# A selective scan laid out as 16 states x 8 channels, with the other stages emitted between its units and the norms' 1/std taken for 8 chunks at once

## Chip, cores, metric

The kernel runs on one core of one Trainium2 chip. The metric is the device time of one launch in microseconds. Medians are over 4 to 9 runs, and the kernel before was run again on the same chip beside every group of experiments (medians 14344 to 14357 us). The engines are PE (TensorE, the matmuls), DVE (VectorE), ACT (ScalarE) and POOL (GpSimd). The granted clock is the share of TensorE's full clock that the trace records; in the traces each stretch of it has either 1.0 ("warm" below) or 0.5 ("cold"), and the numbers between are means over time. "Filling the array" below means 128 rows by 128 columns, the largest size that matmuls have in these traces.

## The reference, cut to what matters

Four images of 96 x 64 x 64 go through four layers: layer 0 is a gated block with a depthwise convolution and a selective scan in four directions, layer 1 a deformable convolution (gathers with bilinear weights), layer 2 a Fourier mixer and a quantized feed-forward block, layer 3 linear attention and another feed-forward block. The scan is:

```python
def selective_scan(u, dts, A, Bs, Cs, D, delta_bias):
    delta = jax.nn.softplus(dts + delta_bias[None, :, :, None])
    ...
    def step(h, inp):
        d_t, u_t, b_t, c_t = inp
        dA = jnp.exp(d_t[..., None] * A)
        h = dA * h + (d_t * u_t)[..., None] * b_t[:, :, None, :]
        y = jnp.einsum('bkdn,bkn->bkd', h, c_t)
        return (h, y)
```

with 192 channels, 16 states, 4 directions and 4096 positions per image.

## The kernel before

It works layer after layer, and in layer 0 image after image. One unit of the scan is one state of 128 channels over 1024 positions (cut):

```python
for n in range(NS):
    bc = sp.tile([128, 2, T], F32, ..., bufs=4)        # B and C of state n, on all partitions
    ...
    nc.sync.dma_start(dst, src.partition_broadcast(dst.shape[0]))
    da = ps.tile([128, T], F32, ..., bufs=2)           # PSUM
    nc.scalar.activation(da, delta, AF.Exp, scale=a_n)
    db = sp.tile([128, T], F32, ..., bufs=2)           # SBUF
    nc.vector.tensor_mul(db, du, bc[:, 0, :])
    nc.vector.tensor_tensor_scan(along(hh), along(da), along(db), first, ALU.mult, ALU.add)
    ...
    nc.gpsimd.tensor_mul(hc, hh, bc[:, 1, :])
    for h in range(T // CH):                           # sum over the states, in PSUM
        nc.tensor.matmul(py[:, hs], lhsT=net.ident, rhs=hc[:, hs], start=(n == 0), stop=(n == NS - 1))
```

The norms take 1/std by a square root, a reciprocal on DVE and a Newton step, once per chunk of 512 positions, on 96 partitions.

Of the kernel before, what the change touches and what calls it, by code (L numbers as in the profile page):

```python
# [9 lines left out]
F32 = mybir.dt.float32  # L10
# [10 lines left out]
L = H * W  # L21
DI, NS, R, KG = 192, 16, 6, 4
D2 = DI - 128
T = 1024
NT = L // T
CH = 512
NCH = L // CH
PW = W + 2
GW = W + 3
GE = GW * GW  # L30

# Columns of "vecs", one small vector per column.
(V_ING, V_INB, V_CBA, V_CBC, V_DTA, V_DTC, V_DSA, V_DSC, V_OGA, V_OBA, V_OGC, V_OBC,
 V_L1B, V_BN2, V_F2B1, V_F2B2, V_BFF, V_F3B1, V_F3B2, V_OMB, NV) = (
    0, 1, 2, 3, 4, 8, 10, 14, 18, 19, 20, 21, 22, 23, 27, 30, 31, 32, 35, 36, 37)


# [1 line left out]
def prepare(x, **w):  # L39
# [14 lines left out]
    for k in range(KG):  # L54
        put(V_DTA + k, w["L0_conv_dt_b"][k, :128])
        put(V_DSA + k, w["L0_conv_Ds"].reshape(KG, DI)[k, :128])
        put(V_DSC + k, w["L0_conv_Ds"].reshape(KG, DI)[k, 128:])
    for p in range(2):
        put(V_DTC + p, np.concatenate([w["L0_conv_dt_b"][2 * p + q, 128:] for q in range(2)]))
# [13 lines left out]
    a["vecs"] = vecs  # L73

    # Layer 0. Tile "a": channels 0..127; tile "c": channels 128..191, twice.
    wi = w["L0_conv_in_proj_w"].T
    a["w_in"] = c(np.concatenate([wi[:, :128], wi[:, 128:192], wi[:, 128:192], wi[:, 192:]], axis=1))
    cw = w["L0_conv_conv_w"].reshape(DI, 9)
    a["cw"] = c(np.stack([cw[:128], np.concatenate([cw[128:], cw[128:]])], axis=1))
    xp = w["L0_conv_x_proj_w"]  # L80
    xp = np.concatenate([xp[:, R:], xp[:, :R]], axis=1).transpose(0, 2, 1)
    a["xp_a"] = c(xp[:, :128].transpose(1, 0, 2))
    a["xp_c"] = c(np.stack([np.concatenate([xp[2 * p, 128:], xp[2 * p + 1, 128:]]) for p in range(2)], axis=1))
    a["dtw"] = c(w["L0_conv_dt_w"].transpose(2, 0, 1))
    al = w["L0_conv_A_logs"].reshape(KG, DI, NS)
    a["al_a"] = c(al[:, :128].transpose(1, 0, 2))
    a["al_c"] = c(np.stack([np.concatenate([al[2 * p, 128:], al[2 * p + 1, 128:]]) for p in range(2)], axis=1))
# [4 lines left out]
    # Layer 1.  # L92
# [5 lines left out]
    a["wdc"] = c(w["L1_conv_weight"].reshape(C, C, 9).transpose(1, 2, 0))  # L98

    # Layers 2 and 3.  # L100
# [13 lines left out]
    # Constants of the shapes alone.  # L114
# [4 lines left out]
    # Centring of 192 channels: from 0..127, and from 128..191 as the lower or the upper half holds them.  # L119
    cen = (np.eye(DI) - 1.0 / DI).astype(f)  # L120
    a["cen_a"] = c(cen[:128])
    a["cen_lo"] = np.concatenate([cen[128:], np.zeros((64, DI), f)])
    a["cen_up"] = np.concatenate([np.zeros((64, DI), f), cen[128:]])
# [6 lines left out]
    def complex_matrix(z):  # L130
        # [k, ..., m] complex -> [(re, im) k, ..., (re, im) m] real
        re = np.concatenate([z.real, z.imag], axis=-1)
        im = np.concatenate([-z.imag, z.real], axis=-1)
        return np.concatenate([re, im], axis=0).astype(f)
# [16 lines left out]
class Net:  # L151
    def __init__(self, ctx, tc, ins):
        self.tc, self.nc, self.ins = tc, tc.nc, ins
        nc = self.nc
        self.const = ctx.enter_context(tc.tile_pool(name="const", bufs=1))
        self.vecs = self.load("vecs", self.const)
        self.ident = self.load("ident", self.const)
        self.cen96 = self.load("cen96", self.const)
        self.grp3 = self.load("grp3", self.const)
        self.mean96 = self.const.tile([96, 96], F32, name="mean96")  # L160
        nc.vector.memset(self.mean96, 1.0 / 96)
        self.eps = self.const.tile([128, 1], F32, name="eps")
        nc.vector.memset(self.eps, 1e-5)
        self.one = self.const.tile([128, 1], F32, name="one")
        nc.vector.memset(self.one, 1.0)

    def load(self, name, pool):
        src = self.ins[name]
        t = pool.tile(list(src.shape), F32, name="w_" + name)
        self.nc.sync.dma_start(t, src)  # L170
        return t
# [3 lines left out]

    def inv_sqrt(self, out, var, tmp, p):
        """out = 1 / sqrt(var + 1e-5) on p partitions. The square root's table is short of
        float32's precision, so a step of Newton's follows."""
        nc, eps = self.nc, self.eps[:p]
        nc.scalar.activation(out, var, AF.Sqrt, bias=eps)  # L180
        nc.vector.reciprocal(out, out)  # L181
        nc.scalar.activation(tmp, out, AF.Square)
        nc.vector.scalar_tensor_tensor(tmp, var, eps, tmp, ALU.add, ALU.mult)  # L183
        nc.gpsimd.tensor_scalar(tmp, tmp, -0.5, 1.5, ALU.mult, ALU.add)  # L184
        nc.gpsimd.tensor_mul(out, out, tmp)  # L185

    def group_norm_stats(self, x, pool, psum, key):
        """Per-channel mean and 1/std of x [96, 4096] over its group of three channels."""
# [6 lines left out]
        gm = psum.tile([C, 512], F32, name=f"gnps{key}", tag="lna")  # L195
# [6 lines left out]
        gv = psum.tile([C, 512], F32, name=f"gnpv{key}", tag="lnb")  # L202
# [4 lines left out]
    def layer_norm(self, out, x, pool, psum, key):  # L207
        """out = (x - mean) / sqrt(var + 1e-5) over the 96 channels (partitions) of x [96, 512]."""
        nc = self.nc
        cen = psum.tile([C, CH], F32, name=f"lnc{key}", tag="lna")  # L210
        nc.tensor.matmul(cen, lhsT=self.cen96, rhs=x, start=True, stop=True)  # L211
        sq = pool.tile([C, CH], F32, name=f"lnq{key}", tag="lnq")
        nc.scalar.activation(sq, cen, AF.Square)
        var = psum.tile([C, CH], F32, name=f"lnv{key}", tag="lnb")
        nc.tensor.matmul(var, lhsT=self.mean96, rhs=sq, start=True, stop=True)  # L215
        sd = pool.tile([C, CH], F32, name=f"lns{key}", tag="lns")
        nw = pool.tile([C, CH], F32, name=f"lnw{key}", tag="lnw")
        self.inv_sqrt(sd, var, nw, C)
        nc.vector.tensor_mul(out, cen, sd)  # L219


@with_exitstack
def layer0(ctx, net, x1):
    """Selective scan over four directions of each image, into x1."""
    tc, nc, ins = net.tc, net.nc, net.ins
    wp = ctx.enter_context(tc.tile_pool(name="l0w", bufs=1))
    w_in = net.load("w_in", wp)
    cw = net.load("cw", wp)
    xp_a = net.load("xp_a", wp)
    xp_c = net.load("xp_c", wp)  # L230
    wo_a = net.load("wo_a", wp)
    wo_c = net.load("wo_c", wp)
    cen_a, cen_lo, cen_up = (net.load(q, wp) for q in ("cen_a", "cen_lo", "cen_up"))
    dtw = wp.tile([2 * NS + R, KG, DI], F32, name="dtw")
    nc.sync.dma_start(dtw[2 * NS :], ins["dtw"])
    pos192 = wp.tile([128, 128], F32, name="pos192")
    nc.vector.memset(pos192, 1.0 / DI)
    # A = -exp(A_logs)
    nega = []
    for name, k in (("al_a", KG), ("al_c", 2)):  # L240
        t = net.load(name, wp)
        nc.scalar.activation(t, t, AF.Exp)
        nc.vector.tensor_scalar_mul(t, t, -1.0)
        nega.append(t)
    # The four directions' skip terms fall on the same pixel.
    dsum = wp.tile([128, 2], F32, name="dsum")
    nc.vector.reduce_sum(dsum[:, 0:1], net.vecs[:, V_DSA : V_DSA + 4], axis=mybir.AxisListType.X)
    nc.vector.reduce_sum(dsum[:, 1:2], net.vecs[:, V_DSC : V_DSC + 4], axis=mybir.AxisListType.X)
    scratch = ctx.enter_context(tc.tile_pool(name="l0d", bufs=1, space=DRAM))
    keep = ctx.enter_context(tc.tile_pool(name="l0keep", bufs=1))  # L250

    for b in range(B):
        xa = keep.tile([128, L], F32, name=f"xa{b}", tag="xa")
        xat = keep.tile([128, L], F32, name=f"xat{b}", tag="xat")
        xc = keep.tile([128, L], F32, name=f"xc{b}", tag="xc")
        ya = keep.tile([128, L], F32, name=f"ya{b}", tag="ya")
        yc = keep.tile([128, L], F32, name=f"yc{b}", tag="yc")
        z_d = scratch.tile([DI, L], F32, name=f"z{b}", tag="z", bufs=2)

        with tc.tile_pool(name=f"l0a{b}", bufs=1) as big, tc.tile_pool(  # L260
            name=f"l0b{b}", bufs=2
        ) as sm, tc.tile_pool(name=f"l0p{b}", bufs=2, space=PSUM) as ps:
            xg = big.tile([C, L], F32, name=f"xg{b}", tag="xg")
            nc.sync.dma_start(xg, ins["x"][b])
            xn_all = big.tile([C, L], F32, name=f"xn{b}", tag="xn")
            pads = []
            for g in range(2):
                t = big.tile([128, PW, PW], F32, name=f"pad{b}_{g}", tag=f"pad{g}")
                nc.gpsimd.memset(t, 0.0)
                pads.append(t)  # L270
            # The depthwise convolution's taps as diagonal matrices.
            diag = big.tile([128, 2, 9, 128], F32, name=f"diag{b}", tag="diag")
            for g in range(2):
                for q in range(9):
                    nc.vector.tensor_scalar_mul(diag[:, g, q, :], net.ident, cw[:, g, q : q + 1])
# [624 lines left out]
```

## Time and profile before

| | before |
|---|---|
| median, us | 14344.2 |
| granted clock, mean | 0.737 |
| busy: PE / DVE / ACT / POOL | 59% / 66% / 26% / 49% |
| scan of one image | 384 units, 4.84 us each (from the starts of DVE's scan instructions) |

The lines that carry this are in the prediction below. One more row of the groups matters later, the sum over the states on PE (its columns are busy us and mean ns of one, then idle time before it and what ended that):

```profile
L473 PE MATMUL py<-hc,w_ident 128*128 128x512 f32 x6144 | 3964.7, 787 | 2956.2 <-POOL hc L470 2954.9
```

These matmuls fill the array, 128 rows by 128 columns (128*128 in the row). In the scan the granted clock is 0.78 although PE is busy only 60% of it.

### The profile page before, as it was taken

To read this page: it belongs to the slowest core of one execution; us is meant where nothing else is said; L and a number is where in the kernel's file an instruction comes from. 1 tells how busy PE (TensorE), PEld (TensorE's weight loads), DVE (VectorE), ACT (ScalarE), POOL (GpSimd) and SP (SyncE) were. 2 spreads that over 40 slices of the span, in tenths; PEclk is the share of its full clock that TensorE was granted. 3 is DMA by queue.
4 is the path that set the end of the run, shared out by engine and by line. 5 is a ranking of instruction groups with operands and counts; after the bars stand their busy time and mean duration, and the time that the engine had idled before them with its cause. 6 is when DMAs were issued, how large, how long until landed. Compare 5 with 4: busy or idle time off the path is not lost. (4 is left out here: it accounts for less than half of the span.)

```text
span 14347.4 us, 74112 instructions
## 1 busy us (share of the span) xinstructions
PE 8526.9 (59%) x24048; PEld 3467.6 (24%) x24048; DVE 9414.3 (66%) x5970; ACT 3702.4 (26%) x5474; POOL 7050.9 (49%) x3392
## 2 busy tenths in 40 slices
PE   7656658665656756656766665624422284848484
PEld 2112112121212212111211211111111161616161
DVE  4999983899995699997499898344444334342424
ACT  3333322333332333332333332101100012121212
POOL 2666662566663366665266665387778501010202
PEclk8777788778778877778887778856655575757575
DMA  2777770677773477775277777334343200000000
GB/s 69 212 219 217 217 215 28 202 214 220 217 222 84 136 216 217 218 213 154 80 216 217 215 220 196 100 117 127 113 149 115 82 1 9 1 9 1 5 1 5
DMA packets 605164, 1962.12 MB, mean 137 GB/s; under 512 B 124492, under 2 KB 127521, under 8 KB 602984
## 3 DMA queue, kind: packets, MB, share of 16 engines
q1 hardware_dynamic: 531048, 1730.82, 41.8%
q0 software_dynamic: 73728, 226.57, 5.4%
q8 instruction: 189, 3.10, 0.1%
q14 instruction: 199, 1.63, 0.0%
HBM read 1890.50 MB, written 66.66 MB: 136 GB/s over the span
## 5 line engine op out<-in xcount | busy, mean ns | idle before, releaser
L470 POOL TENSOR_TENSOR hc<-hh,bc 128x1024 f32<-128x1024 f32 x1536 | 4682.0, 3049 | 2963.8 <-DVE hh L465 2776.7
L473 PE MATMUL py<-hc,w_ident 128*128 128x512 f32 x6144 | 3964.7, 787 | 2956.2 <-POOL hc L470 2954.9
L465 DVE TENSOR_TENSOR_SCAN hh<-da,st,db 128x1024 f32<-128x1024 f32 x1152 | 2702.6, 2347 | 157.4 <-ACT da L460 36.9
L473 PEld LDWEIGHTS py<-hc,w_ident 128*128 128x128 f32 x6144 | 1355.0, 241 | 5510.6 <-POOL hc L470 4291.3
L462 DVE TENSOR_TENSOR db<-du,bc 128x1024 f32<-128x1024 f32 x1536 | 2212.3, 1442 | 118.8 <-DMA bc<-bcd 118.2
L598 POOL DMA_INDIRECT g<-table,idx x1152 | 1677.7, 1456 | 522.1 <-issue 413.4
L460 ACT ACTIVATE da<-de,w_al_a 128x1024 f32<-128x1024 f32 x1024 | 1140.6, 1114 | 736.8 <-DVE hh L465 736.1
L606 DVE TENSOR_TENSOR g<-g,wt 128x3456 f32<-128x3456 f32 x128 | 481.1, 3758 | 1158.2 <-DMA g<-table,idx 1148.7
L615 PE MATMUL ps<-w_ident,s 128*96 128x128 f32 x1152 | 270.1, 408 | 1360.9 <-DVE s L610 1342.0
L468 ACT COPY st<-hh 128x1 f32<-128x1 f32 x1152 | 220.0, 191 | 3132.1 <-DVE hh L465 3132.1
L465 DVE TENSOR_TENSOR_SCAN hh<-da,db 128x1024 f32<-128x1024 f32 x384 | 875.8, 2285 | 49.8 <-ACT da L460 19.1
L442 DVE TENSOR_TENSOR rl<-rl,lw 128x1024 f32<-128x1024 f32 x96 | 246.4, 2566 | 664.3 <-DMA bc<-bcd 472.7
L460 ACT ACTIVATE da<-de,w_al_c 128x1024 f32<-128x1024 f32 x512 | 570.1, 1114 | 399.2 <-DVE hh L465 398.8
L184 POOL TENSOR_SCALAR lnwf<-lnwf 96x512 f32<-96x512 f32 x64 | 39.3, 615 | 1253.2 <-DVE lnwf L183 1253.2
L616 ACT COPY st<-ps 96x512 f32<-96x512 f32 (+1 forms) x384 | 169.8, 475 | 1687.3 <-PE ps L615 1687.1
L184 POOL TENSOR_SCALAR lnw<-lnw 96x512 f32<-96x512 f32 x96 | 59.0, 614 | 1004.7 <-DVE lnw L183 948.5
L181 DVE RECIPROCAL lns<-lns 96x512 f32<-96x512 f32 x96 | 320.9, 3346 | 348.5 <-ACT lns L180 348.5
L615 PEld LDWEIGHTS ps<-w_ident,s 128*96 128x96 f32 x1152 | 197.1, 184 | 1446.2 <-issue 1394.8
L302 PE MATMUL pc<-pad,diag 128*128 128x512 f32 x1152 | 496.5, 593 | 0.1
L805 POOL CAST h8f<-h16f 128x1536 fp8e5<-128x1536 f16 x64 | 93.9, 1468 | 541.9 <-DVE h16f L804 541.9
L430 PE MATMUL pd<-xd,dtw 6*64 6x512 f32 (+1 forms) x512 | 332.5, 879 | 34.0 <-ACT ex L438 34.0
L808 PE MATMUL pof<-h8f,w2q 128*96 128x512 fp8e5 x192 | 91.9, 615 | 353.1 <-POOL h8f L805 353.1
(243 smaller groups left out, 10540.8 us busy)
## 6 DMA issues: line engine op xcount, KB each, us to landing
bc<-bcd SPq DMA_DIRECT2D x1024, 1024.0 KB
bc<-bcd SPq DMA_DIRECT2D x1024, 512.0 KB
table<-pix SPq DMA_DIRECT2D x32, 768.0 KB
g<-table,idx POOLq DMA_INDIRECT x1152, 3.0
x<-xo SPq DMA_DIRECT2D x64, 192.0 KB
z<-zt SPq DMA_DIRECT2D x32, 256.0 KB
bcd<-xd SPq DMA_DIRECT2D x64, 128.0 KB
za<-z SPq DMA_DIRECT2D x32, 256.0 KB
```

What stands on the lines that cost most here:

```text
L181: nc.vector.reciprocal(out, out)
L302: nc.tensor.matmul(pp, lhsT=diag[:, g, q, :], rhs=pads[g][:, r0 + dy : r0 + dy + nr, dx : dx + W], start=(q == 0), stop=(q == 8),)
L430: nc.tensor.matmul(o, lhsT=dtw[2 * NS :, 2 * pr + q, m], rhs=xdbl[q][2 * NS :, hs], start=True, stop=True,)
L442: nc.vector.tensor_add(rl, rl, lw)
L460: nc.scalar.activation(da, delta, AF.Exp, scale=a_n)
L462: nc.vector.tensor_mul(db, du, bc[:, 0, :])
L465: nc.vector.tensor_tensor_scan(along(hh), along(da), along(db), first, ALU.mult, ALU.add)
L470: nc.gpsimd.tensor_mul(hc, hh, bc[:, 1, :])
L473: nc.tensor.matmul(py[:, hs], lhsT=net.ident, rhs=hc[:, hs], start=(n == 0), stop=(n == NS - 1))
L598: nc.gpsimd.indirect_dma_start(out=g[:, k, :], out_offset=None, in_=tables[b % 2], in_offset=bass.IndirectOffsetOnAxis(ap=idx[:, 9 * t + k ...
L606: nc.vector.tensor_mul(g4, g4, w4.unsqueeze(2).to_broadcast([128, 36, C]))
L615: nc.tensor.transpose(pt[:, k, :], s2[:, k0 + k, :], net.ident)
```

## The change

The intent is to fill the half-empty later stages by running them under the scan, to take traffic and DVE work out of the scan, and to remove the 192 reciprocals. The diff cut to its core (it has some 1600 lines; the hand-over buffers in DRAM, the fused convolution and the layers' generators are left out):

```diff
-            db = sp.tile([128, T], F32, ...)
-            nc.vector.tensor_mul(db, du, bc[:, 0, :])
+        nc.sync.dma_start(da, src.unsqueeze(0).to_broadcast([NS, D8, T]))     # 8 channels' delta, 16 times
+        nc.scalar.activation(da, da, AF.Exp, scale=self.al[:, a : a + 1])
+        db = ps.tile([128, 2, CH], F32, ..., bufs=2)                          # PSUM
+        for h in range(2):                                                    # replicate du: 32 rows
+            p0 = 64 * h + 32 * (s // 4)
+            nc.tensor.matmul(db[:, h, :], lhsT=self.rep[p0 : p0 + 32, s % 4, :],
+                             rhs=du[p0 : p0 + 32], start=True, stop=True)
+        nc.vector.tensor_mul(dbf, dbf, bc[:, 0, :])
         nc.vector.tensor_tensor_scan(along(hh), along(da), along(dbf), first, ALU.mult, ALU.add)
         nc.gpsimd.tensor_mul(hc, hh, bc[:, 1, :])
-                    nc.tensor.matmul(py[:, hs], lhsT=net.ident, rhs=hc[:, hs], ...)
+        for h in range(2):                                                    # fold the states: 32 columns
+            q = 2 * h + s // 4
+            nc.tensor.matmul(py[32 * q : 32 * q + 32], lhsT=self.fold[:, s % 4, :],
+                             rhs=hc[:, h * CH : (h + 1) * CH], ...)
...
+            for n, _ in enumerate(l0.scan(b)):            # a step of the other stages after each unit
+                while done * units < total * (n + 1):
+                    step = next(work, None)
...
-        nc.scalar.activation(out, var, AF.Sqrt, bias=eps)
-        nc.vector.reciprocal(out, out)
+        nc.scalar.activation(out, var, AF.Ln, bias=eps)   # var: 8 chunks on 8 partitions
+        nc.scalar.activation(out, out, AF.Exp, scale=-0.5)
```

## The prediction

> **What bounds the kernel now.** I read the busy row and the slices of the page first, then a table of windows by stage, then the groups of instructions, and last the timeline of one steady stretch of the scan.
>
> ```profile
> PE 8526.9 (59%) x24048; PEld 3467.6 (24%) x24048; DVE 9414.3 (66%) x5970; ACT 3702.4 (26%) x5474; POOL 7050.9 (49%) x3392
> ...
> DVE  4999983899995699997499898344444334342424
> ...
> POOL 2666662566663366665266665387778501010202
> PEclk8777788778778877778887778856655575757575
> ```
>
> No engine is full over the whole span, but the digits show three stages: 25 slices with DVE at 9 (layer 0, the scan), then POOL at 7 to 8 with DVE at 4 (layer 1, the gathers), then nothing above 4 (layers 2 and 3). The table of windows, PE, PEld, DVE, ACT, POOL in busy us, gives them sizes: the scan of image 0, layer 1, layers 2 and 3.
>
> ```profile
> 250.00:2130.00 1880.00, 1134.07 (x1775) 364.50 (x1774) 1706.97 (x908) 645.82 (x896) 1163.48 (x382) 0.78 0.74 215
> ...
> 9050.00:11361.00 2311.00, 852.38 (x2576) 385.30 (x2576) 950.48 (x564) 236.16 (x506) 1680.45 (x1164) 0.63 0.42 122
> ...
> 11361.00:14341.00 2980.00, 1913.83 (x12112) 1204.27 (x12112) 1109.78 (x1238) 528.56 (x928) 371.02 (x384) 0.64 0.02 4
> ```
>
> DVE is busy 91% of the scan, 41% of layer 1 and 37% of layers 2 and 3. The stages come one after another: 0 to 9050 us layer 0 (an image takes about 250 before its scan, 1890 in it, 90 after), 2311 for layer 1, 2980 for the rest. So before is a DVE-bound scan of 4 x 1.89 = 7.5 ms, plus 6.8 ms in which DVE works less than half the time. The groups (busy us, mean ns of one):
>
> ```profile
> L470 POOL TENSOR_TENSOR hc<-hh,bc 128x1024 f32<-128x1024 f32 x1536 | 4682.0, 3049 | 2963.8 <-DVE hh L465 2776.7 <-issue 99.5 <-PE py L473 87.7
> ...
> L465 DVE TENSOR_TENSOR_SCAN hh<-da,st,db 128x1024 f32<-128x1024 f32 x1152 | 2702.6, 2347 | 157.4 <-ACT da L460 36.9
> L462 DVE TENSOR_TENSOR db<-du,bc 128x1024 f32<-128x1024 f32 x1536 | 2212.3, 1442 | 118.8 <-DMA bc<-bcd 118.2
> L598 POOL DMA_INDIRECT g<-table,idx x1152 | 1677.7, 1456 | 522.1 <-issue 413.4 <-DVE s L610 104.3 <-DMA g<-table,idx 4.2
> ...
> L181 DVE RECIPROCAL lns<-lns 96x512 f32<-96x512 f32 x96 | 320.9, 3346 | 348.5 <-ACT lns L180 348.5
> ```
>
> One unit of the scan is 128x1024; there are 1536. The timeline shows the steady loop:
>
> ```profile
> 1330.59 1.20 DVE L462 TENSOR_TENSOR db<-du,bc 128x1024 f32<-128x1024 f32 x1
> ...
> 1330.81 3.19 POOL L470 TENSOR_TENSOR hc<-hh,bc 128x1024 f32<-128x1024 f32 x1 [0.35 <-PE py L473]
> 1331.92 2.29 DVE L465 TENSOR_TENSOR_SCAN hh<-da,db 128x1024 f32<-128x1024 f32 x1
> ...
> 1334.13 1.20 DVE L462 TENSOR_TENSOR db<-du,bc 128x1024 f32<-128x1024 f32 x1
> ```
>
> DVE's multiply and scan follow each other with no gap, 3.54 us a unit. POOL's hc takes 3.19 of those 3.54. The mean unit takes 1890/384 = 4.9, because softplus tiles and the sums of y lie between.
>
> [...] hc has a minimum of 2337 ns and a mean of 3049, and the softplus add of line 442 has 1224 at best and 3358 in the median. [...] the trace has 1221 for the sum of y with one operand in PSUM. [...] Here the pairs of line 430, 64 columns each, start 6 to 7 ns apart, and eight take 3.68 us where one of that shape alone takes the cold pace of 0.85. [...] the trace has 1283 each, 252 times.
>
> **The change, part by part.**
>
> *Scan.* The units stay 1536. The multiply now reads du, replicated by PE into PSUM, and B from SBUF, writing PSUM: about 1.22 us in place of 1.44. The scan stays at 2.29 to 2.35. Both then have one SBUF operand, so hc should fall from 3.05 towards 2.34. DVE: 1536 x 1.22 = 1.87 ms (was 2.21) and the scans 3.58 unchanged. The sums of y (114 + 39 us) go. POOL: 1536 x 2.34 = 3.6 ms (was 4.7). DMA: 512 KB per unit for the decay plus 1 MB per 24 units, about 0.57 MB in place of 1; it was 74% busy in the scan, so that limit moves away. PE gets 4 replicating and 4 folding matmuls of 512 columns per unit, where it had 4. At the paces of line 473 (0.43 us warm, 0.85 cold between starts) that is 1.7 us if the pairs run together and 3.4 if not, warm.
>
> *Norms.* 192 reciprocals x 3.35 = 643 us leave DVE and sit on the path of layers 2 and 3; an 8-row logarithm and exponential per 8 chunks takes their place. Newton steps (line 185, 96 x 1.27 = 122 us) leave POOL, the diagonal convolution (1152 matmuls, 497 us) goes into the projection. Table loads rise from 252 to 329: 77 x 1.283 = 99 us on ACT, which is 26% busy.
>
> *Interleaving.* The four scans now follow one another, and image b's scan carries the stages before image b+1 and the out-part, layer 1 and layers 2/3 of image b-1. Exposed stay the start of image 0 and, for image 3, the out-part, layer 1 and layers 2/3.
>
> DVE sum: 3.58 + 1.87 + softplus 0.57 (288 operations, uncontended) + layer 1 0.93 + layers 2/3 0.57 + rest 0.19 = 7.7 ms, about 8.1 with 0.4 for operations with two SBUF operands that still meet POOL. Before it was 9.41. POOL: 3.6 + gathers 1.7 + 0.5 = 5.8. PE: 2.64 + others 3.85 = 6.5 to 7 ms with pairs together, 9.6 with none. ACT about 4.
>
> Time by stage:
> - start to first unit: 0.28 ms (table zeroing of 55 us, the first image's 230 before-part).
> - scan 0: 384 units at 4.9 with 24 of the next image's tiles in it: 1.9 ms.
> - scans 1 and 2: 232 units carrying layers 2/3 at 4.4 us = 1.02; 34 units' pairs in layer 1 at 15.5 us (POOL: two hc, four gather blocks) = 0.52; softplus part 0.44; out-part and next image 0.17; with 7% for waits: 2.3 ms each.
> - scan 3: no next image: 2.1 ms.
> - tail: 0.07 + 0.55 (was 0.58) + 0.62 (was 0.745, less 64 reciprocals' share of 54 us and the Newton steps) = 1.24 ms.
>
> Sum: 0.28 + 1.9 + 4.6 + 2.1 + 1.24 = 10.12. I say **10100 us**. About 5.1 ms of layers 1 to 3 for three images (3 x 1.32 = 4.0) and 3 x 0.34 = 1.0 of the outer parts go behind the scan; the scan pays back some 0.8 for carrying them.
>
> **The rivals.**
> (a) PE becomes the bound. The replication for unit n+2 or n+3 stands in PE's in-order queue behind the fold of unit n, which waits for hc. The ring is hc 2.4, fold, replication, multiply and scan 3.6: with warm pairs about 8.2 us per two units, cold about 9.8, so 4.1 to 4.9 a unit, above DVE's 3.6. If the row or column groups do not overlap, PE needs 3.4 warm and 6.8 cold per unit. For it: PEclk is 5 to 6 in layers 2/3, whose matmuls now sit between. Against: the pairs of line 430 do overlap. It would make 11 to 12 ms.
> (b) The lag falls to one unit, everything serial: hc + fold + replication + multiply + scan is 9 to 10 us a unit, 14 ms or more. The change's instruction order has such a lag in few places (16 to 46 instructions per image), so I give it little.
> (c) Gathers and hand-overs in DRAM block a queue: DVE's weighted sum in layer 1 waited 1149 us for gathered data, and now the scan's next multiply stands behind it[...]. It would add 0.3 to 1 ms.
> (d) Everything hides perfectly, DVE full from first unit to last: 8.1 less the tail's 0.45, plus 0.28 and 1.24, is 9.2 ms.
>
> **Range and chances.** To break even, with 1.5 ms exposed, units would have to take (14.06 - 1.5)/1536 = 8.2 us each, over twice DVE's 3.6: only (b) comes near. (d) sets the low end, (a) with some of (c) the high end: 9300 to 11600. Faster 0.96, same 0.02, slower 0.02.
>
> **What would show it.** In the changed profile: [...] replicating matmuls starting in pairs confirm the groups; no reciprocal group; DVE digits of 8 to 9 from about slice 2 to slice 35, then a tail of about 1.24 ms that looks like before's layers. If DVE is below 75% in the scans and its multiply waits for PE's db, (a) was right; if it waits for DMA, (c). I would be wrong if hc stayed at 3 us, or if a scan unit with nothing in between took over 5 us.

## The result, and the profile after

The changed kernel takes 13937.67 us (13916.41 to 13975.31, 4 runs). Its ratio to the kernel before is 0.9715 (interval 0.9699 to 0.9732). Ratios here are the mean time of one kernel's fast runs over that of the other's of the same rounds, so not quite the quotient of the medians. It is 2.9% faster where about 30% was predicted.

The page of the changed kernel, busy row and slices:

```profile
PE 11335.2 (81%) x32312; PEld 3493.6 (25%) x32312; DVE 7705.0 (55%) x5218; ACT 4003.7 (29%) x5892; POOL 5933.7 (43%) x3060
...
PE   6899999998855899999974699899557999985287
...
DVE  0655566743646566663456666665466666642422
...
PEclk9555555567565566667665566666666566566665
```

DVE's work fell from 9.41 to 7.71 ms, as summed (7.7). But it is no longer the full engine: its digits are mostly 5 and 6 where 8 and 9 were expected. PE has 8s and 9s in the scans, but for the three dips to 4 to 7 where layer 1 lies between the units, and the granted clock is 5 to 7 tenths, lower than the 7 or 8 of before. The groups say the same:

```profile
L532 POOL TENSOR_TENSOR hc<-hh,bc 128x1024 f32<-128x1024 f32 x1536 | 3741.6, 2437 | 5562.3 <-DVE hh L527 4515.2
L516 PE MATMUL db<-du,w_rep 32*128 32x512 f32 x6144 | 3585.6, 982 | 455.5 <-DVE hh L527 409.8
L524 DVE TENSOR_TENSOR db<-db,bc 128x1024 f32<-128x1024 f32 x1536 | 1879.1, 1225 | 3326.3 <-PE db L516 3268.8
L535 PE MATMUL py<-hc,w_fold 128*32 128x512 f32 x6144 | 2682.1, 960 | 1215.3 <-POOL hc L532 1213.3
```

The first and third row are as predicted: hc at 2437 ns where it had 3049, the multiply at 1225. The other two are not. A single one of the narrow matmuls (32 rows, or 32 columns) lasts 960 to 982 ns, and DVE waited 3.27 ms for the replication: with DVE far below 75% in the scans, this is the sign that the prediction gave for its rival (a). The table of windows of the changed kernel (from and to, length, then busy us and instructions of PE, PEld, DVE, ACT, POOL, then clock, DMA share and GB/s) has these rows: a stretch of scan 0; the next image's before-part, layer 1, and layers 2 and 3 under scan 1; then, alone at the end, the out-part, layer 1, layers 2 and 3 of the last image.

```profile
1200.00:2300.00 1100.00, 1068.76 (x1802) 219.42 (x1798) 653.65 (x377) 413.87 (x542) 432.76 (x184) 0.53 0.45 118
3047.00:3739.00 692.00, 612.29 (x1214) 148.61 (x1214) 342.62 (x233) 355.14 (x464) 229.13 (x100) 0.68 0.40 111
3739.00:4638.00 899.00, 512.69 (x1408) 181.94 (x1408) 539.97 (x302) 174.95 (x291) 628.82 (x376) 0.62 0.50 134
4638.00:6149.00 1511.00, 1393.93 (x5111) 485.04 (x5111) 977.47 (x697) 409.48 (x624) 583.58 (x259) 0.65 0.43 110
12402.00:12630.00 228.00, 169.05 (x208) 32.66 (x208) 19.63 (x31) 38.22 (x58) 19.83 (x16) 0.67 0.23 62
12630.00:13268.00 638.00, 217.61 (x788) 129.66 (x788) 234.31 (x144) 62.94 (x135) 407.88 (x297) 0.64 0.38 108
13268.00:13925.00 657.00, 535.16 (x3092) 317.80 (x3092) 152.90 (x255) 123.73 (x220) 41.98 (x34) 0.64 0.08 25
```

PE is busy 97% of the first stretch at a clock of 0.53, and 92% under layers 2 and 3. Only in the layer-1 stretch is no engine near full. The timeline of the changed kernel in scan 0 shows the clock at work:

```profile
1499.82 1.92 PE L535 MATMUL py<-hc,w_fold 128*32 128x512 f32 x4
1501.67 2.07 PE L516 MATMUL db<-du,w_rep 32*128 32x512 f32 x2
1503.67 2.08 PE L361 MATMUL pc<-pad,wc 96*128 96x512 f32 x2
1503.78 1.23 DVE L524 TENSOR_TENSOR db<-db,bc 128x1024 f32<-128x1024 f32 x1 [5.85 <-PE db L516]
...
1505.68 1.92 PE L535 MATMUL py<-hc,w_fold 128*32 128x512 f32 x4
...
1507.53 3.84 PE L361 MATMUL pc<-pad,wc 96*128 96x512 f32 x8
...
1511.30 1.05 PE L535 MATMUL py<-hc,w_fold 128*32 128x512 f32 x4
```

PE hardly rests here. The four fold instructions of a unit start as two pairs 6 to 7 ns apart, so the column groups do run together; yet they take 1.92 us. Eight instructions of the next image's convolution, of 96 rows by 128 columns, come at 1507.53. After the first of them their pace is 0.43 us where it was 0.85, since the trace's clock goes from 0.5 to 1.0 at 1507.84, and the same fold right after them takes 1.05. (What raised the clock at that moment, this view does not show.)

The replication is different. It too has four instructions a unit, but the line at 1501.67 has only two of them, which run one after the other, with other matmuls before and behind. Where four stand together, as here under layers 2 and 3, they take no longer than these two:

```profile
5001.92 2.08 PE L516 MATMUL db<-du,w_rep 32*128 32x512 f32 x4
```

Counted over the trace's records, 3020 of the fold's 3072 possible pairs start within 20 ns of each other, but only 1956 of the replication's 3072. So a third of the replication ran without a partner, which costs PE time besides the low clock. By stage (scan starts and ends from DVE's scan instructions):

| us | predicted | measured |
|---|---|---|
| start to first unit | 280 | 369 |
| scan 0 | 1900 | 2473 |
| scans 1 and 2, each | 2300 | 3301, 3299 |
| scan 3 | 2100 | 2921 |
| tail | 1240 | 1548 |

### The profile page after: what moved, and what is told of

Read it like the earlier page. It is cut to its first block, busy times and chain, and to the rows that moved or that the text cites. A ratio compares the mean times of both kernels' runs of the same rounds, so it can differ in the third digit from the quotient of the medians.

```text
span 13924.8 us, 93384 instructions
## 1 busy us (share of the span) xinstructions
PE 11335.2 (81%) x32312; PEld 3493.6 (25%) x32312; DVE 7705.0 (55%) x5218; ACT 4003.7 (29%) x5892; POOL 5933.7 (43%) x3060
## 5 line engine op out<-in xcount | busy, mean ns | idle before, releaser
L532 POOL TENSOR_TENSOR hc<-hh,bc 128x1024 f32<-128x1024 f32 x1536 | 3741.6, 2437 | 5562.3 <-DVE hh L527 4515.2
L516 PE MATMUL db<-du,w_rep 32*128 32x512 f32 x6144 | 3585.6, 982 | 455.5 <-DVE hh L527 409.8
L524 DVE TENSOR_TENSOR db<-db,bc 128x1024 f32<-128x1024 f32 x1536 | 1879.1, 1225 | 3326.3 <-PE db L516 3268.8
L535 PE MATMUL py<-hc,w_fold 128*32 128x512 f32 x6144 | 2682.1, 960 | 1215.3 <-POOL hc L532 1213.3
L512 ACT ACTIVATE da<-da,w_al 128x1024 f32<-128x1024 f32 x1536 | 1759.6, 1148 | 2128.6 <-DMA da<-de 2028.8
L516 PEld LDWEIGHTS db<-du,w_rep 32*128 32x128 f32 x6144 | 897.6, 269 | 2520.8 <-issue 2164.8
L535 PEld LDWEIGHTS py<-hc,w_fold 128*32 128x32 f32 x6144 | 282.3, 133 | 3089.9 <-POOL hc L532 2129.2
L361 PE MATMUL pc<-pad,wc 96*128 96x512 f32 x1152 | 636.0, 706 | 0.6
L772 PE MATMUL pd<-st,wdc 96*96 96x256 f32 x1152 | 359.2, 473 | 1.4 <-ACT st L766 0.5
L425 PE MATMUL pd<-xd,dtw 7*64 7x512 f32 (+1 forms) x512 | 344.3, 994 | 19.0 <-ACT ex L433 14.3
L361 PEld LDWEIGHTS pc<-pad,wc 96*128 96x128 f32 x1152 | 240.8, 219 | 401.5 <-issue 379.7
```

Source lines behind the costliest of these rows:

```text
L361: nc.tensor.matmul(pp, lhsT=wc[:, q, g * 128 : (g + 1) * 128], rhs=pad[:, r0 + dy : r0 + dy + NR, dx : dx + W], start=(q == 0), stop=(q == 8),
L425: nc.tensor.matmul(o, lhsT=dtw[2 * NS :, 2 * pr + q, m], rhs=xdbl[q][2 * NS :, hs], start=True, stop=True,)
L512: nc.scalar.activation(da, da, AF.Exp, scale=self.al[:, a : a + 1])
L516: nc.tensor.matmul(db[:, h, :], lhsT=self.rep[p0 : p0 + 32, s % 4, :], rhs=du[p0 : p0 + 32], start=True, stop=True,)
L524: nc.vector.tensor_mul(dbf, dbf, bc[:, 0, :])
L535: nc.tensor.matmul(py[32 * q : 32 * q + 32], lhsT=self.fold[:, s % 4, :], rhs=hc[:, h * CH : (h + 1) * CH], start=alone and s % 4 == 0, st ...
```

## The experiments

Theory A: PE is the bound, since the narrow matmuls leave the granted clock low and all of PE's work, the scan's and the interleaved stages', runs at the slow pace. Rivals: B, the clock is low for another reason (the short waits); C, the scan unit is slow by itself; D, the ring fold, replication, multiply, scan sets the period; E, the transfers do; G, in the layer-1 stretch POOL's queue does; H, there the streams take turns on DVE.

| run | median us | ratio | clock | PE busy ms | unit of scan 0, us |
|---|---|---|---|---|---|
| changed kernel | 13938 | 0.9715 | 0.638 | 11.34 | 6.44 |
| full | 13834 | 0.9636 | 0.887 | 10.76 | 6.06 |
| repfull | 12555 | 0.8736 | 0.858 | 9.59 | 4.99 |
| foldfull | 14602 | 1.0165 | 0.772 | 11.30 | 6.75 |
| seq | 14618 | 1.0173 | 0.613 | 12.04 | 6.47 |
| room | 13969 | 0.9725 | 0.634 | 11.39 | 6.44 |
| latefold | 13729 | 0.9573 | 0.651 | 11.22 | 6.30 |
| repfull_late | 12364 | 0.8618 | 0.872 | 9.50 | 5.00 |
| nodu | 13535 | 0.9436 | 0.637 | 7.94 | 6.35 |
| bf16 | 11545 | 0.8054 | 0.613 | 7.38 | 4.59 |
| bfold_repfull | 11918 | 0.8306 | 0.826 | 8.82 | 4.84 |
| hc_l1dve | 12069 | 0.8414 | 0.876 | 9.52 | 4.99 |
| best | 11237 | 0.7829 | 0.667 | 7.42 | 4.52 |
| best_n | 11310 | 0.7885 | 0.614 | 7.40 | 4.62 |

All gave correct results.

### Filling the array: full, repfull, foldfull, and their control room

The weights get zeros outside their 32 rows or columns, so the same number of matmul instructions gives the same result with 128 rows (replication) or 128 columns (fold). The pairs then no longer run together: at the high clock four of full's fold took 1.98 us (at 2209.92 of its timeline) and four of repfull's replication 1.88 (at 3510.50), where four of repfull's narrow fold took 1.05 (at 3512.31).

```diff
-                lhsT=self.rep[p0 : p0 + 32, s % 4, :], rhs=du[p0 : p0 + 32],
+                lhsT=self.rep[:, p0 // 32, s % 4, :],  rhs=du,                      # full, repfull
-                py[32 * q : 32 * q + 32], lhsT=self.fold[:, s % 4, :],
+                py, lhsT=self.fold[:, 120 - 32 * q - 8 * (s % 4) : 248 - 32 * q - 8 * (s % 4)],   # full, foldfull
```

> Both small matmuls of the scan fill the array: the replication takes 128 rows (weights with zeros outside its 32) and the fold 128 columns (zeros outside its 32), so the pairs no longer run together and a unit has 8 matmuls one after another. Same result. Theory A (the narrow matmuls leave the clock low; PE is the bound because of that): the granted clock in the scan rises from 0.53-0.66 to 0.8 or more, a unit's 8 matmuls take about 3.5 us at 0.43 each, where the pairs took 4.0 cold, every other matmul between units is up to twice as fast, and the whole kernel comes to about 12000 us. Rival B (the clock is low for another reason, the short waits between units): the clock stays below 0.65, 8 matmuls take 6.8 us, the kernel 15500 us or more.

> Only the replication fills the array. A: the clock rises part of the way, about 0.7; replication 1.72 us warm instead of 2.08 cold, the kernel about 13000 us. B: replication 3.4 us a unit, the kernel about 15500 us.

> Only the fold fills the array. A: clock about 0.7, fold 1.72 us warm instead of 1.92 cold, the kernel about 13000 us. B: fold 3.4 us a unit, the kernel about 15500 us.

> Control for the two runs with 128-row replication: only the shared buffers that made room for their larger weights (the gate rows and the norm's scratch take the buffers of the squares), with the changed kernel's narrow matmuls. Every theory: 13938 us within 1%, clock 0.64. If it were faster by itself, the gain of the 128-row replication would be smaller than it seemed.

Repfull is 9.9% faster than the changed kernel (12555 against 13938), and its control, which shares the same buffers with narrow matmuls, is not faster at all (13969). Page and groups of repfull:

```profile
PE 9592.7 (76%) x32312; PEld 3448.5 (27%) x32312; DVE 7731.8 (62%) x5218; ACT 4011.5 (32%) x5892; POOL 5957.3 (47%) x3060
...
PEclk9899999997777999998777899998678999966675
...
L517 PE MATMUL db<-du,w_rep 128*128 128x512 f32 x6144 | 3450.2, 675 | 499.8 <-DVE hh L528 449.4 <-issue 29.4 <-DVE gndv L209 4.7
...
L536 PE MATMUL py<-hc,w_fold 128*32 128x512 f32 x6144 | 1831.1, 672 | 1525.6 <-POOL hc L533 1519.7
```

The replication itself hardly gained: 3450 us one after another, where it had 3586 with 64% of its pairs together. What gained is what was not touched. The fold is as narrow as it was, and went from 2682 to 1831 us, 960 to 672 ns each; the remaining matmuls went from 5.07 (11.335 - 3.586 - 2.682) to 4.31 ms. That is the clock, 0.64 to 0.86, so B falls. (Widening also ends the running together of pairs, so width and this are not told apart by any run.)

Full and foldfull missed what A expected of the time. They raised the clock too (0.887, 0.772), but not cheaply:

```profile
L536 PE MATMUL py<-hc,w_fold 128*128 128x512 f32 x6144 | 3504.0, 698 | 1838.3 <-POOL hc L533 1834.2 <-ACT st L531 0.2
```

This is full's fold: 3504 us against repfull's 1831 at nearly the same clock, because its pairs no longer run together. In foldfull it is 4441 us at 0.77. So what counts is PE's time, instructions times pace less overlap, more than the clock as such: the replication is worth widening, the fold is not. It is not the whole account of these two runs, though. Foldfull's PE is busy no longer than the changed kernel's (11.30 and 11.34 ms), yet it is 4.8% slower (14602 against 13938), and in this stretch of full's scan 0 the clock is 1.00 and no engine is full, with PE at 85% and 6.1 us a unit:

```profile
1000.00:1600.00 600.00, 508.60 (x1112) 199.08 (x1110) 350.54 (x199) 176.07 (x240) 241.27 (x107) 1.00 0.43 115
```

A fold that takes longer may also hold up the replication behind it, as in rival D's ring. That this is the cause was not tried: the late fold below was run with the narrow fold alone.

### Emitting the stages after each scan: seq

```diff
-            for n, _ in enumerate(l0.scan(b)):
-                while done * units < total * (n + 1): ...
+            for _ in l0.scan(b):
+                pass
             for step in work:
```

> The other stages come after each image's scan instead of between its units; nothing else changes. Theory A says that the interleaving hides next to nothing since PE, the bound, does all of it one after another: scans alone at 4.0 (PE cold) to 4.9 us a unit (the ring fold, replication, multiply, scan), 6.1 to 7.5 ms, and the other stages about 1.6 ms an image, together 12600 to 13900 us, no slower than the changed kernel's 13938. Rival C (interleaving does hide the stages, and the scan unit is slow by itself, at 6.4 us): 384 x 6.4 x 4 = 9.8 ms + 6.4 ms = 16200 us.

14618 us lies between the two expectations, and the total does not decide, since my edit did not do what I meant. PE of seq inside scan 0, where only the scan's own matmuls should be:

```profile
2009.52 2.07 PE L516 MATMUL db<-du,w_rep 32*128 32x512 f32 x2
2011.52 2.08 PE L361 MATMUL pc<-pad,wc 96*128 96x512 f32 x2
2013.53 1.94 PE L491 MATMUL py<-ad,w_ident 128*32 128x512 f32 x8
```

L361 is the next image's convolution, which this edit emits after the scan. Its matmuls stand between the units all the same, so the order of emission is not the order on the engine. Of the order itself seq shows only that the emission of the change is 4.7% better than this one (ratios 1.0173 and 0.9715). But one stretch of it answers rival C. Early in scan 1 little else lies between the units, and 464 of PE's 572 us are the scan's own replication and fold:

```profile
3000.00:3600.00 600.00, 572.11 (x1094) 110.69 (x1094) 404.05 (x240) 172.30 (x250) 275.60 (x121) 0.58 0.57 142
```

A unit takes 5.3 us there (from the starts of DVE's scan instructions), with PE busy 95%. So the unit by itself is slow, though not the 6.4 us of C, and it is PE at the low clock that is full. The prediction had named just this as a sign of being wrong: "if a scan unit with nothing in between took over 5 us".

### The ring: latefold, repfull_late

The fold of a unit is emitted after the next unit, so that a replication need not stand behind it.

```diff
-                        self.unit(...)
+                        late = self.unit(...)      # returns its fold
+                        if fold:
+                            fold()
+                        fold = late
```

> The fold of a unit is emitted one unit later, so that the replication of the unit after next need not stand behind it. Theory A (PE's time at the low clock is the bound): PE does the same work, 13938 us within 1.5%. Rival D (the ring fold, replication, multiply, scan sets the period): up to 1.5 us less a unit, 12000 to 12500 us.

> 128-row replication and the late fold together. At the high clock PE is no longer full (76%), so what is left of the ring should show here if anywhere: D: scan units of image 0 from 4.99 us to about 4.2, the kernel 11800 us. A: nothing left to gain in PE, 12555 us within 1.5%.

The gain is 1.5% on the changed kernel (13938 to 13729) and 1.5% on repfull (12555 to 12364); units of scan 0 go from 6.44 to 6.30 and from 4.99 to 5.00. In the changed kernel's trace PE stood over 0.5 us before a fold, waiting for hc, 37 times (51 us in all) while the replication right behind that fold had its operand and a free buffer. What this edit takes out of the ring is worth about 200 us, not the 1.5 us a unit that D asked for.

### Taking the replication off PE by DMA: nodu

```diff
-            nc.tensor.matmul(db[:, h, :], lhsT=self.rep[...], rhs=du[p0 : p0 + 32], ...)
-        nc.vector.tensor_mul(dbf, dbf, bc[:, 0, :])
+        nc.sync.dma_start(du, self.du_d[b][k][c0 : c0 + D8, ts].unsqueeze(0).to_broadcast([NS, D8, T]))
+        nc.vector.tensor_mul(dbf, du, bc[:, 0, :])
```

> The replication leaves PE: du comes replicated by a broadcast DMA, as the decay does, and DVE reads it from SBUF; the fold stays narrow. PE loses 3.6 ms of its 11.3, its clock may stay low. A: DVE's wait for the replication (3269 us) goes, hc returns to about 3.0 us since the multiply has two SBUF operands again, the kernel 11500 to 12500 us. Rival E (the transfers are the bound: with 512 KB more a unit the traffic is what it was before, about 1 MB a unit): units at 5 us or more, the multiply waits for DMA, 13000 us or more. The layer-1 stretch should stay at 11.9 us a unit in any case, since it did so at both clocks.

PE fell to 7.94 ms, but the kernel only to 13535 us, and scan 0 stayed at 6.35 us a unit. The window of scan 0 and the wait of the multiply in nodu:

```profile
1600.00:2200.00 600.00, 296.75 (x596) 37.40 (x596) 433.12 (x227) 229.31 (x302) 304.21 (x108) 0.52 0.87 210
```

```profile
DVE db L516 <- DMA du<-du: 1253.2, 445, 20.3
```

PE is at 49%, and the transfers at 87% with 210 GB/s: rival E took the place of the wait that was removed. The multiply also went back to 1607 ns and hc to 2749. Alone this run would have spoken against A; it could not, because it put in a new bound.

### Operands of 2 bytes at the low clock: bf16, bfold_repfull

The scan's two matmuls get operands of 2 bytes (du and hc rounded to bf16; less exact, still correct by the comparison with the reference), so one instruction in place of two (3072 in place of 6144 for each of the two). The matmuls stay narrow in bf16; in bfold_repfull only the fold is changed, on top of repfull_late.

```diff
-        hc = sp.tile([128, T], F32, ...)
+        hc = sp.tile([128, T], BF16, ...)
-        du = sp.tile([128, CH], F32, ...)
+        du = sp.tile([128, CH], BF16, ...)          # and rep, fold copied to BF16
```

> The changed kernel's narrow matmuls with operands of 2 bytes (du and hc in bf16, so the result is less exact, perhaps out of tolerance)[...], with the clock left as low as it is. It takes PE's load away without touching the clock. Theory A (PE's time is the bound of the scan, whatever its clock): PE busy falls by some 4.5 ms from 11.3, the wait of the multiply for the replication mostly goes, scan units of image 0 fall from 6.44 to about 4.8, the stretch with layers 2/3 from 6.5 to about 4.9, the kernel to 11500-12300 us. If PE's time is not the bound: no more than 3% faster than 13938.

> 128-row replication in fp32, late fold, and the fold alone in bf16: tells whether PE still sets the time at the high clock. A: the fold's 1851 us fall to about 500, and the kernel from 12364 to about 11700 us; if only the clock's state matters, no change within 1.5% (or slower, if the clock falls with the lighter fold).

```profile
1200.00:2050.00 850.00, 505.47 (x1257) 104.51 (x1257) 789.42 (x464) 463.70 (x618) 548.76 (x222) 0.52 0.69 179
```

This is the stretch of bf16 in scan 0. The clock is as low as before (0.52), PE is down to 59%, and DVE is at 93%: the engine that was meant to be the bound. The kernel takes 11545 us, 17% less than the changed one, with units at 4.59 us. The wait of the multiply for the replication went from 3269 to 1438 us:

```profile
DVE db L532 <- PE db L524: 1437.8, 398, 144.3
```

Part of this may be the pairs: 1467 of the replication's 1536 possible ones now start together. The 4.5 ms by which PE's time was to fall were the estimate, as were the 500 us for bfold_repfull's fold; PE's time fell by 3.96 ms (11.34 to 7.38), the replication's from 3586 to 914 us and the fold's from 2682 to 891. So the miss is PE's time, reached here with the clock untouched and in repfull with fp32 operands and the same number of instructions. At the high clock the fold in bf16 is still worth 3.6% (12364 to 11918): PE still set much of the time there.

### The layer-1 stretch: hc_l1dve

```diff
-        nc.gpsimd.tensor_mul(hc, hh, bc[:, 1, :])
+        (nc.vector if net.sampling else nc.gpsimd).tensor_mul(hc, hh, bc[:, 1, :])   # sampling: layer 1's steps
```

> On the version with 128-row replication and late fold (12364 us): while layer 1's steps lie between the units, the multiply by C goes to DVE, so that it does not stand behind nine gathers in POOL's queue. Theory G (in this stretch POOL's queue is the bound, its order rather than its sum): the stretch's 12.0 us a unit fall to 9 to 10, 239 units in three images, so 500 to 700 us less, about 11750 us. Rival H (the gathers with their weighted sums and the scan take turns on DVE, and DVE gets 1.2 us more per unit): the stretch stays at 12 us or grows.

Repfull_late's stretch under scan 1, and the same stretch of hc_l1dve:

```profile
3059.00:3965.00 906.00, 517.43 (x1448) 195.63 (x1448) 551.91 (x313) 208.19 (x332) 646.71 (x380) 0.75 0.51 137
```

```profile
3053.00:3873.00 820.00, 512.78 (x1448) 198.65 (x1447) 591.22 (x387) 207.59 (x332) 500.52 (x305) 0.78 0.55 152
```

From 12.2 to 10.9 us a unit, and 295 us for the kernel (12364 to 12069), about half of what G expected. POOL's queue is part of it (in repfull's timeline a scan ended at 3517.90 and its hc started at 3525.20, after the gathers before it), and H, which expected no gain, is not the whole. What holds the rest, where POOL has 61% and DVE 72%, is not settled.

### Together: best, best_n

The edits of bf16, latefold and hc_l1dve, with 128-row replication (best) or narrow (best_n).

> All that helped, together: du and hc in bf16 [...], 128-row replication, late fold, multiply by C on DVE while layer 1 lies between. Now PE has 1536 x (0.43 + 0.21) of scan work at the high clock. If the clock still matters [...] (for the other stages' matmuls between the units), the clock is 0.8 or more and the kernel 11000 us or less; if not, it is no faster than the same with narrow replication. Either way below 11545.

> The same with the narrow, paired replication of the changed kernel. Theory: clock about 0.61 as in the bf16 run, so the stages between the units run at the low clock: 11250 us, 250 to 400 us more than with 128 rows. If the clock is no longer worth anything, both agree within 1%.

Best takes 11237 us, 0.7829 of the kernel before and 19% less than the changed kernel; best_n 11310. The 0.43 + 0.21 us a unit of the expectation are the estimate; measured is PE's sum, 7.42 and 7.40 ms. The expected clock of 0.8 did not come: bf16 replication of 128 rows lifts it to 0.667 only, against 0.614. So the width is worth 0.65% with operands of 2 bytes.

## Why the prediction was wrong, by its own steps

- **DVE's and POOL's sums** held: 7.71 ms for 7.7 (8.1 with the allowance for POOL), hc 2437 ns for "towards 2.34" us, the multiply 1225 for 1.22. POOL 5.93 for 5.8, ACT 4.0 for about 4, table loads 329 as counted (1283 ns each in both traces, 252 of them before). That hc would come near its least time in before, 2337 ns, was the estimate from what DVE reads beside it, and the runs bear it out: hc went from 3049 to 2437 ns in the mean (3184 to 2350 in the median) when DVE's operations of the scan had one operand in PSUM, and back to 2749 in the mean in nodu, where the multiply read both from SBUF.
- **The reading of the slices** was too rounded: of the "25 slices with DVE at 9" 15 have a 9, the others 3 to 8, since each image's other parts lie between the scans. The windows, on which the sums rest, were read rightly.
- **PE's sum is the step that failed**: "1.7 us if the pairs run together and 3.4 if not, warm", and "6.5 to 7 ms with pairs together". The fold's pairs do run together and two thirds of the replication's do, but mostly not warm. A unit took 2.33 + 1.75 = 4.1 us (3586 and 2682 over 1536), the other matmuls 5.07 ms where the sum had 3.85, and PE was busy 11.3 ms. Had all the replication's pairs run together at the pace they had (3586 us over 4188 separate starts), it would have taken about 1.7 us a unit in place of 2.33, an estimate. So of the 2.4 us by which a unit's 4.1 exceed the forecast 1.7, about 0.6 are lost pairs and most of the rest is the clock. I took the pace of line 473, whose matmuls fill the array, for matmuls of 32 rows or 32 columns, and took the granted clock of before for granted after.
- **Rival (a) named the low clock and was given 11 to 12 ms.** It was sized as the scan's ring alone, 4.9 us a unit. Almost alone the unit took 5.3 (seq); with the interleaved stages, which go through PE's queue at the same low clock, 6.4 to 6.5. The ring, which I worked out for it, was tested by the late fold, and that is worth 1.5%.
- **"Against: the pairs of line 430 do overlap"** answered only half of the doubt. The other half was the clock, and the same line gave a warning that was passed over: eight of those pairs' matmuls took 3.68 us, the cold pace.
- **The gain of the interleaving** needed an engine mix that leaves PE free. Under layers 2 and 3 I had 4.4 us a unit and it took 6.5; with PE relieved (bf16) it took 4.75.
- **The layer-1 stretch** was mis-sized: 15.5 us for two units, measured 24, at either clock. Three images of it make some 2.8 ms, and it is still 2.6 ms in best.
- **The tail** was 1548 for 1240 us: the out-part took 228 us alone instead of 70, layer 1 638 instead of 550, layers 2 and 3 657 for 620 (745 before). The reciprocals went as planned. Whether the hand-over in DRAM or the norm of four chunks at once made the out-part longer was not tried, nor why the start took 369 us for 280.
- **Rival (c)** was not the cause in the changed kernel: DVE's sum waited 455 us for gathered data, less than the 1149 of before. Rival (d), DVE full, is what bf16 comes near to in scan 0.

## What to carry to other kernels

When matmuls are cut into narrow tiles, or put in to move data, size them at the slow clock (here 0.85 us from start to start of f32 matmuls over 512 positions, where the fast one has 0.43) unless a trace shows the fast one for matmuls of that very shape, and add the other stages' matmuls at that clock too. Here PE was busy 97% of 1100 us at a granted clock of 0.53. With the same number of matmul instructions, the clock of the whole kernel went from 0.638 to 0.858 when the replication was widened from 32 to 128 rows, to 0.772 when the fold was widened from 32 to 128 columns, and to 0.887 with both; width and the end of the pairs are not told apart by these runs. Count in the trace how many of the pairs really start together (here 1956 of the replication's 3072). A stage hidden under another one is hidden only as far as every engine's sum, taken at the pace it will run at, leaves room (here PE was 92% busy under layers 2 and 3). If an engine is full at a low clock, try wider tiles and operands of 2 bytes before reordering: here reordering gave 1.5%, the wider replication 10% (the wider fold alone cost 4.8%), operands of 2 bytes 17%. The gains do not add up: with operands of 2 bytes, width gave 0.65%.
